# A four-layer graph network: layer 2's accumulators and row products change PSUM tiles, and four edge checks change layers

## The chip, the cores and the metric

The kernel runs on one core of one Trainium2 chip. The metric is the device time of one execution in microseconds; the time before is the median of three runs. A profiled execution gives the trace from which single waits are read.

The engines are called by these names: TensorE (PE in the profile; PEld is its weight load), VectorE (DVE), ScalarE (ACT), GpSimd (POOL) and SyncE (SP), whose queue issues the loads.

## The reference

Node features `x` (4096 x 64) pass through four layers over one adjacency matrix `adj` (4096 x 4096, zeros and ones). Each layer's result is added to its input and normalised by row.

```python
# layer 0: mean over neighbours and self, a linear map of [x, mean], relu, row norm
# layers 1 and 3: hyperbolic attention; for every pair (i, j) a weight
#   sigmoid(left[i] + right[j]) * adj[i, j] times a function of the pair's distance
# layer 2:
support = input @ weight
mask = (adj != 0).astype(support.dtype)
rank = jnp.cumsum(mask, axis=1)
deg = rank[:, -1:]
k = jnp.minimum(deg, float(MAX_NEIGH))
pos = rank - (deg - k)
w = mask * jnp.where(pos > 0, DECAY ** (k - pos), 0.0)
out = w @ support + bias
# after each layer
x = _layernorm(x + layer(x, adj, ...), axis=-1)
```

In layer 2 an edge is thus weighted by two to the minus the number of edges that stand behind it in its row.

## The kernel before

The host hands `adj` over in a blocked order. The 4096 target rows are four groups of 1024 (`GROUPS`, taken in the order 3, 2, 1, 0); the 4096 sources are 32 blocks of 128 (`BLOCKS`, taken from 31 down to 0). `load(s, g)` (L702) brings the edges of group s with two blocks, g from 15 down to 0: one megabyte, 128 partitions by 2 by 1024 fp32, into one of six `edges` buffers. Every layer reads all 64 loads, so the matrix is read four times. The matmuls read the upper bf16 half of each fp32 edge.

**Checks.** The fast path is only valid if every entry is 0 or 1 in the form that it relies on. Each of the 64 loads is therefore checked once, by one VectorE operation over the whole buffer (`check`, L844, 128 x 2048 fp32), which holds the buffer until it is done. `checked_later(s, g)` says in which layer: where it is false, in layer 0 (output `junk`), where it is true, in layer 2 (output in a `t` buffer). Half of the loads of each group go to either layer. Groups 3 and 2 check the loads g = 0, 1, 2, 3, 5, 7, 9, 11 in layer 2; groups 1 and 0 the odd g.

**Row work.** When a group's edges have been summed, the group's 1024 rows go through "row work": the layer's end (`end_0`, `move`, `end_2`), the norm (`norm_rows`) and the preparation of the next layer's operands (`prepare`: casts L931 to L933 on ScalarE, transposes L978, copies out of PSUM L982, the attention product L991, its readers L1001 and L1004, and small operations). These are generators in queues; `tick()` advances them between the blocks of the next group's pass. The order on TensorE and ScalarE in layers 0 and 2 is that of the program (`manual_schedule`); the order on VectorE, GpSimd and SyncE is the planner's.

**PSUM.** [...] After layer 0 the pools are: `aux` (one bank), `z` (three buffers of two banks) and `acc` (one buffer, one bank). Row work takes its PSUM space with `take()`: by turns from `aux` and, where `spare` offers one, from a second place.

**Layer 2.** It has three passes: a wide one over groups 3 and 2 together (`wide_pass`) and two narrow ones over group 1 and group 0 (`narrow_pass`). For each block, `count` (L1641) adds to a running count in a z tile with two matmuls per 512 columns, `weights_of` (L1648) turns the count into weights with ScalarE's exponential, and `add_up` (L1653, wide) or `add` (L1607, narrow) multiplies the weights with the block's supports and accumulates. In a narrow pass each half of 512 rows has its own z tile and its own accumulator, so that one half's exponential runs beside the other half's matmuls. At the end of a pass ScalarE copies the two accumulators to SBUF (L1684), and `end_2` carries them on: transposed or stacked into PSUM (L1134, L1550), read by L1556 and L1560.

Layer 2 takes one of the three z tiles for its whole length:

```python
weighed = [None]
third_z = z_tile()

def of_third(dtype, shape):
    t = third_z[:, W:]
```

The first half of `third_z` is the second accumulator, `accs = [ps.tile([P, W], F32, name="acc"), third_z[:, :W]]`; the second half is row work's second place (`spare.append(of_third)`). The profile names this tile `z`, as it does the other z tiles.

Layer 3 (`attention`, `attend`) follows at once: its loop is L1098, L1101, L1104 on TensorE, the sigmoid L1113 and the square L1116 on ScalarE, L1119 and L1121 on VectorE and the sum L1076 into `acc`.

Of the kernel before, what the change touches and what calls it, by code (L numbers as in the profile page):

```python
# [10 lines left out]
F32 = mybir.dt.float32  # L11
# [8 lines left out]
P = 128  # L20
# [3 lines left out]
W = 512  # L24
# [36 lines left out]
def gnn_stack_kernel(  # L61
# [509 lines left out]
    def stream(fits):  # L571

        with ExitStack() as st:

            def pool(name, bufs=1, **kw):
                return st.enter_context(tc.tile_pool(name=name, bufs=bufs, **kw))
# [7 lines left out]
            GROUPS = tuple(reversed(range(NW)))  # L584
# [31 lines left out]
            def tick(n):  # L616
                for _ in range(n):
                    place[1] += 1
                    mark(False)
                    for queue in queues:  # L620
                        while queue and queue[0][1] <= place[1]:
                            wait = next(queue[0][0], None)
                            if wait is None:
                                queue.pop(0)
                                continue
                            queue[0][1] = place[1] + wait
                            if wait:
                                break
                    mark(True)
# [13 lines left out]
            def need(tag):  # L643
                while tag not in done:
                    assert any(queues), tag
                    tick(1)
# [58 lines left out]

            def checked_later(s, g):

                return g in (0, 1, 2, 3, 5, 7, 9, 11) if s in GROUPS[:2] else g % 2 == 1

            def grp(name, bufs=None):  # L710
                kw = {"bufs": bufs} if bufs else {}
# [2 lines left out]
            def nums(name, n=WB):  # L714
                return row.tile([P, n], F32, name=name)
# [638 lines left out]
            with ExitStack() as lp:  # L1354
                own = lp.enter_context(tc.tile_pool(name="m0_own", bufs=1))
                sb = lp.enter_context(tc.tile_pool(name="m0_sb", bufs=2))
                ps = lp.enter_context(tc.tile_pool(name="m0_ps", bufs=6, space=PSUM))
# [91 lines left out]
                with tc.manual_schedule(engines=FIXED):  # L1449
                    for s in GROUPS:  # L1450
# [3 lines left out]
                        for g in reversed(range(NB // 2)):  # L1454
# [3 lines left out]
                            if not checked_later(s, g):  # L1458
                                check(s, g, a, own.tile([P, 2, WW], BF16, name="junk"))
# [44 lines left out]
            ps = pool("p_ps", 1, space=PSUM)  # L1504

            def z_tile():
                return ps.tile([P, WW], F32, name="z", bufs=3)
# [63 lines left out]
            def wide_pass(two):  # L1571

                zs = [z_tile() for _ in two]

                accs = [ps.tile([P, W], F32, name="acc"), third_z[:, :W]]
                behind, lag = [None, None], []
                for g in reversed(range(NB // 2)):
                    edges = [load_2(s, g) for s in two]
                    need((2, 2 * g // WB))
                    for k in (1, 0):  # L1580
                        j = 2 * g + k
                        w = sb.tile([P, 2, WW], F32, name="sq").bitcast(BF16)[:, :, :WW]
                        for i, edge in enumerate(edges):
                            here = edge[:, k * WW : (k + 1) * WW]
                            count(zs[i], behind[i], here, j, WW)
                            behind[i] = here
                            weights_of(zs[i], WW, w[:, i])
                            if i == 1:
                                for of, acc in enumerate(accs if lag else ()):
                                    add_up(acc, *lag[of])  # L1590
                                lag = [(j, w[:, n, :W], w[:, n, W:]) for n in range(2)]
                            if two[0] != GROUPS[0] or j < BLOCKS[4]:
                                tick(1)
                for of, acc in enumerate(accs):
                    add_up(acc, *lag[of])
                return [[acc] for acc in accs]

            def narrow_pass(s):

                zs = [z_tile() for _ in range(2)]  # L1600
                accs = [ps.tile([P, W], F32, name="acc"), third_z[:, :W]]
                behind, lag = [None, None], [None, None]

                def add(h):
                    if lag[h] is not None:
                        j, w = lag[h]
                        nc.tensor.matmul(  # L1607
                            accs[h], halves[:, j, :], w,
                            start=j == BLOCKS[0], stop=j == BLOCKS[-1],
                        )  # L1610

                for g in reversed(range(NB // 2)):
                    edge = load_2(s, g)
                    for k in (1, 0):
                        j = 2 * g + k
                        w = sb.tile([P, 2, WW], F32, name="sq").bitcast(BF16)[:, 0, :WW]
                        for h in range(2):
                            here = edge[:, k * WW + h * W : k * WW + (h + 1) * W]
                            count(zs[h], behind[h], here, j, W)
                            behind[h] = here  # L1620
                            add(h)
                            part = w[:, h * W : (h + 1) * W]
                            weights_of(zs[h], W, part)
                            lag[h] = (j, part)
                        tick(1)
                for h in range(2):
                    add(h)
                return [accs]

            def load_2(s, g):  # L1630
                a, edge = load(s, g)
                if checked_later(s, g):
                    junk = sb.tile([P, 2, WW], F32, name="t", bufs=3).bitcast(BF16)
                    check(s, g, a, junk[:, 0, :].rearrange("p (b i) -> p b i", b=2))
                return edge

            def count(z, behind, here, j, n):
                for lhs, rhs in ((pass_by, behind), (enter, here)):
                    for h in range(0, n, W):
                        if rhs is not None:  # L1640
                            nc.tensor.matmul(  # L1641
                                z[:, h : h + W], lhs, rhs[:, h : h + W],
                                start=j == BLOCKS[0], stop=True, skip_group_check=True,
                            )

            def weights_of(z, n, w):

                weighed[0] = nc.scalar.activation(w, z[:, :n], AF.Exp, bias=-(OFF_EDGE + CUT) * LN2, scale=-LN2)  # L1648

            def add_up(acc, j, *ws):  # L1650
                for part in range(2):
                    for h, w in enumerate(ws):
                        nc.tensor.matmul(  # L1653
                            acc[h * D : (h + 1) * D, :],
                            halves[:, j, part * D : (part + 1) * D], w,
                            start=j == BLOCKS[0] and part == 0,
                            stop=j == BLOCKS[-1] and part == 1,
                        )

            weighed = [None]  # L1660
            third_z = z_tile()

            def of_third(dtype, shape):
                t = third_z[:, W:]
                if dtype == F16:
                    return t.bitcast(F16)
                n = int(np.prod(shape[1:]))
                if len(shape) == 2:
                    return t[:, :n]
                names = "abc"[: len(shape) - 1]  # L1670
                return t[:, :n].rearrange(
                    "p (%s) -> p %s" % (" ".join(names), " ".join(names)),
                    **dict(zip(names, shape[1:])),
                )

            with tc.manual_schedule(engines=FIXED):
                spare.append(of_third)

                for some in (GROUPS[:2], GROUPS[2:3], GROUPS[3:]):
                    accs = wide_pass(some) if len(some) == 2 else narrow_pass(some[0])  # L1680
                    for s, of in zip(some, accs):
                        sums = [row.tile([P, W], F32, name="sums", bufs=2) for _ in of]
                        for to, acc in zip(sums, of):
                            nc.scalar.copy(to, acc)  # L1684
                        later(end_2(s, sums))
                spare_ends()
# [16 lines left out]
            t, g = nums("m1", 1), nums("g1", 1)  # L1703
# [21 lines left out]

    fits = const.tile([P, 1], F32, name="fits")
    stream(fits)

    n_fit = const.tile([1, 1], I32, name="n_fit")
    with tc.tile_pool(name="fit_ps", bufs=1, space=PSUM) as ps:  # L1730
        t = ps.tile([1, P], F32, name="fit_t")
# [52 lines left out]
```

## Time and profile before

| what | value |
|---|---|
| median of three runs | 1076.47 us (1074.18 to 1076.71) |
| the profiled execution | 1073.46 us, span 1071.7 us |
| mean granted TensorE clock | 0.975 |
| busy: PE, DVE, ACT, POOL | 985.7, 919.6, 754.4, 272.3 us |
| layer 0, about | 0 to 184 us |
| layer 1, about | 184 to 513 us |
| layer 2, about | 513 to 720 us (narrow passes from 610 and from 666) |
| layer 3 and the end, about | 720 to 1072 us |
| a check (L844), layer 0 and layer 2 | 2.28 us each, 32 in either layer |

The span runs from the first to the last instruction of the profiled execution; the execution's own time is 1.8 us longer. Single durations and waits come from that one execution; the time to beat is the median. In lists of waits a line says which engine and line waited, for which engine and line, for how long in total, how often and how long at most. In timelines a line is start, duration, engine, line, operation, output and inputs, and in brackets the idle time before it with what ended it. TensorE's durations overlap, since matmuls are pipelined: the spacing of their starts is what counts.

### The profile page before, as it was taken

The numbers are of one execution on the slowest core, as the hardware profiler recorded it, in microseconds if no ns is written. First come the engines' busy times: TensorE is split into PE (matmuls) and PEld (weight loads), VectorE is DVE, ScalarE is ACT, GpSimd is POOL, SyncE is SP. The second block draws the span as 40 slices with busy tenths as digits, with TensorE's granted clock in tenths as the row PEclk, the third lists the DMA queues.
The fourth block names the chain that finished last, engine by engine and source line by source line (L and its number), as shares of the span: only waits on it lengthen the run. The fifth ranks groups of instructions, "written<-read, shape, count | busy, mean of one in ns | idle before, by whom it ended". The sixth has DMA issues, their size and how long they took to land.

```text
span 1071.7 us, 13656 instructions
## 1 busy us (share of the span) xinstructions
PE 985.7 (92%) x4845; PEld 401.4 (37%) x4845; DVE 919.6 (86%) x1501; ACT 754.4 (70%) x877; POOL 272.3 (25%) x649
## 2 busy tenths in 40 slices
PE   4997998789999999999999989998899999999980
PEld 2454554333333333333333334443333333333320
DVE  7676888999999999999485698829999999999976
ACT  0013122879988889888677778898898888898850
POOL 0011211010044515425500021101102444444162
PEclk9999999989999999999999999999999999999985
DMA  9999999645666656657699979896465666666300
GB/s 340 387 424 356 381 416 377 256 167 197 235 205 227 229 202 210 227 192 240 226 358 324 385 282 342 292 327 223 148 237 194 245 221 209 239 230 229 135 1 24
DMA packets 38580, 271.62 MB, mean 253 GB/s; under 512 B 4710, under 2 KB 4710, under 8 KB 5734
## 3 DMA queue, kind: packets, MB, share of 16 engines
q1 hardware_dynamic: 37728, 270.03, 69.2%
q8 instruction: 40, 0.66, 0.2%
q10 hardware_dynamic: 774, 0.63, 0.2%
q14 instruction: 38, 0.31, 0.1%
HBM read 269.58 MB, written 1.05 MB: 253 GB/s over the span
## 4 chain that ended last, share of the span: by engine, by line
PE 61%; DVE 25%; ACT 6%; DMA 3%; POOL 2%; issue 2%; ACTq 0%; SPq 0%; POOLq 0%; DVEq 0%
PE acc L1076 17%; PE z L1641 9%; PE z L1098 8%; PE z L1104 7%; PE z L1101 7%; DVE t L1119 6%; DVE t L1121 6%; PE acc L1465 4%; DVE junk L844 3%; DMA edges<-in_adj_dram 2%; ACT sq L1648 2%; PE acc L1653 2%; ACT sq L1116 1%; PE z L1653 1%; ACT sig L1113 1%
## 5 line engine op out<-in xcount | busy, mean ns | idle before, releaser
L1119 DVE SCALAR_TENSOR_TENSOR t<-z,sig 128x1024 f32<-128x1024 f32 x256 | 309.8, 1219 | 12.8 <-ACT sq L1116 10.9
L1121 DVE SCALAR_TENSOR_TENSOR t<-sq,t 128x2048 f32<-128x2048 f32 x128 | 295.2, 2307 | 0.2
L1116 ACT ACTIVATE sq<-z 128x1024 f32<-128x1024 f32 x256 | 254.2, 1021 | 56.6 <-PE z L1104 21.6
L1113 ACT ACTIVATE sig<-left_b,right 128x1024 f32<-128x1024 f32 x256 | 286.9, 1149 | 5.3 <-DVE t L1119 4.5
L1076 PE MATMUL acc<-t,xe 128*64 128x512 f32 x1024 | 260.0, 614 | 10.6 <-DVE t L1121 9.7
L1098 PE MATMUL z<-edges,two_i 128*128 128x512 bf16 x512 | 200.9, 392 | 5.5 <-DVE t L1119 5.4
L1104 PE MATMUL z<-dst,src 74*128 74x512 f16 x512 | 194.7, 380 | 0.0
L1101 PE MATMUL z<-lo_hi,hi_lo 128*128 128x512 f16 x512 | 193.8, 378 | 0.0
L1648 ACT ACTIVATE sq<-z 128x512 bf16<-128x512 f32 (+1 forms) x192 | 137.8, 741 | 45.3 <-PE z L1641 44.7
L1076 PEld LDWEIGHTS acc<-t,xe 128*64 128x64 f32 x1024 | 64.3, 137 | 140.5 <-issue 106.0
L1465 PE MATMUL acc<-edges,first 128*128 128x512 bf16 x256 | 80.8, 397 | 17.4 <-DMA edges<-in_adj_dram 17.2
L1098 PEld LDWEIGHTS <-two_i 128*128 128x128 bf16 x512 | 50.3, 98 | 120.5 <-issue 74.5
L1641 PE MATMUL z<-edges,pass_by 128*128 128x512 bf16 x248 | 87.2, 391 | 4.9 <-ACT sq L1648 4.6
L844 DVE SCALAR_TENSOR_TENSOR t<-edges 128x2048 bf16<-128x2048 f32 x32 | 73.0, 2287 | 21.4 <-DMA edges<-in_adj_dram 21.0
L1641 PE MATMUL z<-edges,enter 128*128 128x512 bf16 x256 | 88.8, 389 | 0.0
L844 DVE SCALAR_TENSOR_TENSOR junk<-edges 128x2048 bf16<-128x2048 f32 x32 | 73.1, 2284 | 9.0 <-DMA edges<-in_adj_dram 8.8
L1465 PE MATMUL acc<-edges,third 128*65 128x512 bf16 x256 | 80.4, 396 | 0.0
L1104 PEld LDWEIGHTS <-src 74*128 74x128 f16 x512 | 49.2, 96 | 72.1 <-issue 9.2
L1101 PEld LDWEIGHTS <-hi_lo 128*128 128x128 f16 x512 | 50.2, 98 | 60.6 <-issue 14.6
L901 POOL TENSOR_TENSOR sq<-z 128x512 f32<-128x512 f32 x8 | 16.2, 2024 | 168.4 <-DVE z L900 147.3
L1184 POOL TENSOR_TENSOR w_att<-x,u 128x512 f32<-128x512 f32 x6 | 12.7, 2122 | 139.7 <-ACT u L1179 139.7
L1465 PEld LDWEIGHTS <-first 128*128 128x128 bf16 x256 | 24.3, 98 | 45.1 <-issue 16.2
(402 smaller groups left out, 987.3 us busy)
## 6 DMA issues: line engine op xcount, KB each, us to landing
edges<-in_adj_dram SPq DMA_DIRECT2D x256, 1024.0 KB, 4.9
x<-in_x_dram SPq DMA_DIRECT2D x4, 256.0 KB
out_dram<-x ACTq DMA_DIRECT2D x2, 256.0 KB
out_dram<-x SPq DMA_DIRECT2D x2, 256.0 KB
w_sb<-in_L_gnn_W_dram ACTq DMA_DIRECT2D x1, 32.0 KB, 4.7
w_twice<-in_L_gnn_weight_dram ACTq DMA_DIRECT2D x2, 16.0 KB, 8.7
given<-in_L_gnn_b_dram ACTq DMA_DIRECT2D x1, 0.2 KB
given<-in_L_gnn_bias_dram ACTq DMA_DIRECT2D x1, 0.2 KB
```

What stands on the lines that cost most here:

```text
L844: V.scalar_tensor_tensor(junk, a, 0.0, a, ALU.not_equal, ALU.not_equal, accum_out=odd[:, n : n + 1])
L1076: it = nc.tensor.matmul(acc[h * D : (h + 1) * D, :], xe[:, j, :], t[:, k, h * W : (h + 1) * W], start=j == BLOCKS[0], stop=j == BLOCKS[-1],)
L1098: nc.tensor.matmul(half, two_i, edge[:, at : at + W], start=True, stop=False)
L1101: nc.tensor.matmul(half, hi_lo[:, of], lo_hi[:, to], start=False, stop=False)
L1104: last = nc.tensor.matmul(half, src[:, of], dst[:, to], start=False, stop=True)
L1113: nc.scalar.activation(sig, left_b, AF.Sigmoid, bias=right[:, j : j + 1])
L1116: nc.scalar.activation(sq[:, k], zp, AF.Square, bias=ROOT + OFF, scale=-1.0 / UNIT)
L1119: V.scalar_tensor_tensor(t[:, k], zp, 0.0, sig, ALU.max, ALU.mult)
L1121: V.scalar_tensor_tensor(t, sq, HIGH**2, t, ALU.add, ALU.mult)
L1465: nc.tensor.matmul(accs[h][:m], lhs[:, j, :], edge[:, at : at + W], start=j == BLOCKS[0], stop=j == BLOCKS[-1],)
L1641: nc.tensor.matmul(z[:, h : h + W], lhs, rhs[:, h : h + W], start=j == BLOCKS[0], stop=True, skip_group_check=True,)
L1648: weighed[0] = nc.scalar.activation(w, z[:, :n], AF.Exp, bias=-(OFF_EDGE + CUT) * LN2, scale=-LN2)
```

## The change

Three things are edited. `checked_later` returns for groups 1 and 0 what it returned for groups 3 and 2. Both accumulators of a pass are the two halves of `third_z`. Row work's second place is a tile of its own, `row_bank`, allocated once for layer 2 in the `acc` buffer, and `of_third` hands out views of it.

```diff
             def checked_later(s, g):
 
-                return g in (0, 1, 2, 3, 5, 7, 9, 11) if s in GROUPS[:2] else g % 2 == 1
+                return g in (0, 1, 2, 3, 5, 7, 9, 11)
...
                 zs = [z_tile() for _ in two]
 
-                accs = [ps.tile([P, W], F32, name="acc"), third_z[:, :W]]
+                accs = [third_z[:, :W], third_z[:, W:]]
                 behind, lag = [None, None], []
...
                 zs = [z_tile() for _ in range(2)]
-                accs = [ps.tile([P, W], F32, name="acc"), third_z[:, :W]]
+                accs = [third_z[:, :W], third_z[:, W:]]
                 behind, lag = [None, None], [None, None]
...
             weighed = [None]
             third_z = z_tile()
+            row_bank = ps.tile([P, W], F32, name="acc")
 
             def of_third(dtype, shape):
-                t = third_z[:, W:]
+                t = row_bank
                 if dtype == F16:
                     return t.bitcast(F16)
```

For groups 1 and 0 this means: of layer 2's checks, those of loads 15 and 13 move to layer 0, and of layer 0's, those of loads 2 and 0 move to layer 2. The number of checks in either layer stays 32.

## The prediction

> **What bounds the kernel now.** I read the page for the order of the stages, then the table of stretches for each stage, then the list of waits between 510 and 725 us, and then the timelines of TensorE, VectorE and ScalarE around the waits that looked wrong. Layer 0 ends near 184 us, layer 1 near 513, layer 2 near 720. The change touches layers 0 and 2. The stretches first (length, busy time of PE, PEld, DVE, ACT, POOL, then TensorE clock, DMA share, GB/s): three passes of layer 0, then layer 2's wide pass and its two narrow passes.
>
> ```profile
> 54.00:97.00 43.00, 39.00 (x227) 21.81 (x226) 34.88 (x92) 7.90 (x14) 8.72 (x9) 1.00 0.95 382
> 97.00:141.00 44.00, 39.79 (x241) 22.82 (x241) 35.63 (x104) 11.18 (x19) 6.65 (x9) 1.00 0.96 392
> 141.00:184.00 43.00, 40.77 (x256) 23.89 (x254) 35.87 (x109) 10.24 (x19) 6.80 (x9) 1.00 0.97 395
> 510.00:610.30 100.30, 98.55 (x582) 37.33 (x580) 61.80 (x126) 69.66 (x77) 16.70 (x53) 1.00 0.86 319
> 610.30:666.00 55.70, 49.62 (x251) 22.76 (x248) 49.38 (x177) 43.66 (x75) 10.12 (x16) 0.97 0.87 318
> 666.00:720.30 54.30, 50.60 (x290) 24.57 (x289) 30.41 (x100) 48.11 (x83) 4.75 (x8) 1.00 0.88 313
> ```
>
> Layer 0 is bound by its loads. The wide pass is TensorE back to back. The narrow passes are TensorE's too, but with holes: six matmuls per block at 0.2255 us from start to start are 1.353 us, 43.3 us for 32 blocks, against 54 to 56 us taken; row products and short waits on ScalarE fill most of the rest. The first narrow pass alone has a mean clock under 1.00. The waits of layer 2 (who waited, for whom; total, times, longest) and the place of the largest on TensorE and VectorE:
>
> ```profile
> PE z L1607 <- DVE z L1560: 3.4, 1, 3.4
> PE z L1607 <- ACT lo_hi L982: 0.5, 2, 0.2
> PE z L1607 <- ACT dst L982: 0.4, 2, 0.2
> DVE lr L1001 <- ACT sums L1684: 18.0, 1, 18.0
> ```
>
> ```profile
> 623.01 0.39 PE L1641 MATMUL z<-edges,enter 128*128 128x512 bf16 x1
> 626.85 0.59 PE L1607 MATMUL z<-sq,halves 128*128 128x512 bf16 x1 [3.44 <-DVE z L1560]
> 627.23 0.63 PE L1641 MATMUL z<-edges,pass_by 128*128 128x512 bf16 x1
> ```
>
> ```profile
> 625.96 0.42 DVE L1556 SCALAR_TENSOR_TENSOR z<-z,given_b 128x256 f32<-128x256 f32 x1
> 626.38 0.42 DVE L1560 SCALAR_TENSOR_TENSOR z<-z,given_b 128x256 f32<-128x256 f32 x1
> ```
>
> L1607 adds block sums into the first half of `third_z`; L1560 reads a row product out of the second half. They share no number, yet the add waits for the read. The same holds six more times: L1607 waits for L982's copy exactly where that copy reads a z tile, never where it reads `aux`. In the other direction L1001, reading L991's row product in the second half, starts only after the sums' copy of the first half. So waits follow the whole tile.
>
> **What the Trainium skill says.** "PSUM — Partial Sum Buffer", section "PSUM bank collisions raise a hardware error", wants engines kept apart by bank and quadrant; the two halves are 512 fp32 columns each, a bank each, so these waits are wider than the chip asks. "TensorE: Matmul & The Clock Gate", "What's actually happening", has TensorE at half rate after an idle window of about 3.4 us: the trace agrees, the matmuls after the 3.44 us hole start 0.43 us apart instead of 0.2255. "PSUM", "Engine vs sequencer instructions", calls ScalarE's queue a strict FIFO: here three casts at 633.11 keep the next block's exponential waiting and TensorE idles 1.16 us.
>
> **The change, part by part.** It adds and removes no instruction; it moves two PSUM buffers and four checks.
>
> *Tiles.* Both accumulators now lie in `third_z`, row products in the `acc` bank.
> (1) The hole at 623 goes: 3.44 us, and the slow stretch after it: 626.85 to 630.16 for eight matmuls is 3.31 us, at 0.2255 it is 1.80, so 1.5 us more. TensorE sets the pass here; all 4.9 counts. What is late next: ScalarE's casts (L931 to L933), in a fixed order. With the hole gone they come due at 633.11 less 4.9 to 5.1, about 628.1. They need y, which VectorE finished at 631.47. One check ahead of it (615.16, 2.29 us) moves away, so y is there at about 629.3. ScalarE, and the exponentials queued behind the casts, with TensorE waiting for those, lose about 1.0 us; bounds 0.3 (y took 1.54 us beside a GpSimd product, 0.69 elsewhere) and 3.5 (VectorE's order unchanged).
> (2) The six waits of 0.22 us, 1.35 in all: without them TensorE runs a little ahead into the exponential that stands behind the same copy. I take half, 0.7; bounds 0 and 1.35.
> (3) At the end, lr (723.21) and seven small operations stand ahead of layer 3's first L1119 (724.14), though its sigmoid was ready at about 722.6. The row product was made by about 719. Free of the sums' copy, this 0.9 us falls into VectorE's idle time before 722.6, and VectorE is full from 738 to 760, so 0.9 counts; bounds 0 (ScalarE still sets the second L1119) and 1.4.
> (4) The price: a copy of one accumulator now waits for the last add of the other too. At 610.17 the first copy started some 0.3 us before the other's adds ended; the narrow pass's exponentials follow in ScalarE's order: minus 0.3; at the other two pass ends the copies are late anyway. Bounds 0 and 1.
> The first row product in `acc` comes at about 532, the copy that frees it ends at 518.4, and layer 3's first add into `acc` (730.16) is after the last read: nothing at either end.
>
> *Checks.* Passes 1 and 0 move their checks of loads 15 and 13 from layer 2 to layer 0 and those of loads 2 and 0 the other way, 2.28 us each on both sides. In layer 2 the later ones fall beside work: at 650 to 666 VectorE already checked the next pass's loads 15 and 13 (661.5, 663.7), which now go, and after 704.58 it idled 18 us. They hold no buffer that TensorE is not still reading (SyncE's waits there: 188 us for TensorE, 1.2 for checks). In layer 0 they do hold buffers:
>
> ```profile
> SPq L702 <- DVE junk L844: 60.2, 16, 6.7
> SPq L702 <- PE acc L1465: 10.1, 11, 1.9
> ```
>
> That is SyncE's queue from 97 to 184 us: every later load stands behind a load whose buffer waits for a check. How much of it starves the DMA? The shares above leave 5%, 4% and 3% of 43 or 44 us: 2.2, 1.8 and 1.3 us. Pass 2 already has the new pattern and loses 0.4 to 0.9 us more than the others. So I charge 0.4 + 0.9 = 1.3 us for passes 1 and 0. Against it, the last check of layer 0 (182.14 to 184.36) no longer stands before L1428 (184.57), for which TensorE waited 0.93 us at 185.14: plus 0.9. Net minus 0.4. Bounds: minus 9.1 (four checks of 2.28 us, each delaying a load in full) and plus 1.2 (nothing but the end).
>
> **Sum**: 4.9 - 1.0 + 0.7 + 0.9 - 0.3 - 0.4 = 4.8 us. The profiled execution took 1073.46 us (span 1071.7, 1.8 around it), so 1068.7 on its scale; the median of the runs is 1076.47, 3.0 above that execution, so **1071.7 us**. A measurement of this kernel tells 0.3%, 3.2 us, from no change.
>
> **Rivals.**
> *The wait moves to the casts.* VectorE's work before y is not shortened, for instance because other ready work takes the freed place; y stays at 631.47 and ScalarE waits 3.5 us in place of 1.0. For it: VectorE is busy nearly without a break from 624 to 666. Against: one check less stands ahead. Gain 4.8 - 2.5 = 2.3, 1074.2 us: within 0.3%.
> *Layer 0 starves (slower).* In passes 1 and 0 the checks of loads 15 and 13 come ahead of the previous pass's row work, whose chain runs serially through GpSimd; the checks behind it free their buffers later, and the loads of a load-bound stage come late. Full price 9.1 us: 1071.7 - 0.4 + 9.1 = 1080.4 us. It decides from a loss of about 5.2 us in layer 0 on, and exceeds 0.3% from 8.4. For it: the 60.2 us above. Against it: pass 2, and VectorE's holes of 6.0 us at 94.7 and 3.6 at 141, where a check of load 15 fits.
> *More is gained.* The casts wait 0, layer 0 gets the plus 1.2, lr its 1.4, the short waits their 1.35: 4.8 + 1.0 + 1.6 + 0.5 + 0.65 = 8.6, 1067.9 us.
> *The change does nothing*, if waits did go by bank: the seven waits speak against it; I give it no chance of its own.
>
> **How the numbers follow.** Forecast 0.53, more gained 0.12, casts 0.20, layer 0 0.15. The forecast's own range is 1069.5 to 1074.5; its upper edge, 0.04, belongs to no change. Faster 0.61, same 0.24, slower 0.15. The range goes from 1067.0, below the larger gain, to 1079.0, past the casts and a partly starved layer 0; it leaves out about 0.15.
>
> **What would show it.** Right: no wait of L1607 for L1560 or L982; the first narrow pass near 51 us at clock 1.00; a new ScalarE wait of about 1 us at L931 for y; lr before layer 3's first L1119; DMA share of 0.95 in the passes at 97 and 141 us and no check within 4 us of layer 0's end. Wrong: layer 0 over 3 us longer, the hole at another instruction of the narrow pass, or L1607 still waiting for row work.

## The result, and the profile after

The changed kernel takes 1071.84 us in the median (22 runs, 1067.79 to 1079.21), the kernel before, run beside it, 1076.59 (22 runs). The ratio is 0.996, with a 95% interval of 0.9945 to 0.9974: faster by 0.4%, 2.8 to 5.9 us. A second comparison of the same two kernels gave 0.9967 (0.995 to 0.9983). The profiled execution has a span of 1067.3 us against 1071.7, and both kernels' executions are 1.8 us longer than their spans.

The table of stretches of the changed kernel, in the columns used before. The three passes of layer 0 are cut where they were; the wide pass and the two narrow ones are cut where they now begin and end.

```profile
54.00:97.00 43.00, 38.66 (x223) 21.80 (x225) 35.17 (x93) 7.84 (x14) 8.72 (x9) 1.00 0.96 388
97.00:141.00 44.00, 39.68 (x239) 22.92 (x242) 36.06 (x105) 10.95 (x19) 8.74 (x9) 1.00 0.94 381
141.00:184.00 43.00, 40.38 (x250) 23.67 (x252) 36.53 (x109) 10.50 (x19) 8.59 (x9) 1.00 0.97 395
509.60:610.20 100.60, 98.11 (x572) 37.37 (x582) 59.50 (x124) 69.37 (x77) 16.71 (x53) 1.00 0.85 320
610.20:661.20 51.00, 47.41 (x243) 22.32 (x247) 43.59 (x158) 43.85 (x76) 6.07 (x16) 1.00 0.95 336
661.20:714.90 53.70, 50.05 (x284) 24.63 (x288) 39.33 (x130) 48.01 (x81) 3.46 (x8) 1.00 0.91 324
```

The first narrow pass is where the time came from: 51.0 us at a clock of 1.00, where it took 55.8 at 0.97. The wide pass and layer 0 are nearly what they were; only the pass of layer 0 from 97 us has a lower DMA share, 0.94 against 0.96. All of TensorE's waits between 500 and 720 us, weight loads apart:

```profile
PE z L1641 <- ACT sq L1648: 6.0, 7, 1.4
PE acc L1076 <- DVE t L1121: 1.1, 1, 1.1
PE z L1607 <- ACT sq L1648: 0.5, 2, 0.3
PE acc L1319 <- ACT x_t L1312: 0.2, 1, 0.2
PE aux L1550 <- ACT sums L1685: 0.2, 1, 0.2
```

L1607 waits neither for L1560 nor for L982 any more. What it waits for is its own input, the exponential. VectorE at the place of the old hole:

```profile
621.92 2.29 DVE L844 SCALAR_TENSOR_TENSOR t<-edges 128x2048 bf16<-128x2048 f32 x1
624.26 0.42 DVE L1556 SCALAR_TENSOR_TENSOR z<-acc,given_b 128x256 f32<-128x256 f32 x1
624.67 0.42 DVE L1560 SCALAR_TENSOR_TENSOR z<-acc,given_b 128x256 f32<-128x256 f32 x1
...
626.75 0.69 DVE L928 TENSOR_TENSOR y<-x,ym 128x512 f32<-128x512 f32 x1
627.35 0.69 DVE L900 TENSOR_TENSOR z<-z,n_m 128x512 f32<-128x512 f32 x1
```

The row product now comes from `acc`, and TensorE doesn't wait for the read. In this pass one check stands ahead of `y` where there were two (615.16 and 622.15 in the kernel before), and `y` is done at 627.44, while ScalarE reaches its casts (L931) at 628.31: they don't wait.

The profiled execution's 4.4 us, stage by stage (start of the stage to start of the next, taken from the same instructions in both traces):

| stage | before | after | difference |
|---|---|---|---|
| up to layer 1's first L1119 | 194.02 | 193.66 | -0.36 |
| layer 1, to layer 2's first count | 315.99 | 315.95 | -0.04 |
| wide pass, to the first copy of its sums | 100.16 | 100.59 | +0.43 |
| first narrow pass, to its first copy | 55.84 | 50.95 | -4.89 |
| second narrow pass, to its last add | 53.89 | 53.37 | -0.52 |
| to layer 3's first L1119 | 4.24 | 4.15 | -0.09 |
| layer 3, to its last L1121 | 312.38 | 313.65 | +1.27 |
| rest | 35.18 | 34.98 | -0.20 |

Layer 2 gives 5.0 us. One thing was not foreseen: layer 3 takes 1.27 back, though the change touches nothing there.

### The profile page after: what moved, and what is told of

Read it like the earlier page. It is cut to its first block, busy times and chain, and to the rows that moved or that the text cites. A ratio compares the mean times of both kernels' runs of the same rounds, so it can differ in the third digit from the quotient of the medians.

```text
span 1067.3 us, 13569 instructions
## 1 busy us (share of the span) xinstructions
PE 982.1 (92%) x4760; PEld 403.2 (38%) x4845; DVE 920.2 (86%) x1501; ACT 754.3 (71%) x877; POOL 270.8 (25%) x649
## 4 chain that ended last, share of the span: by engine, by line
PE 66%; DVE 22%; ACT 5%; DMA 2%; POOL 2%; issue 2%; ACTq 0%; SPq 0%; POOLq 0%
PE acc L1076 17%; PE z L1641 11%; PE z L1101 8%; PE z L1098 7%; PE z L1104 7%; DVE t L1119 7%; DVE t L1121 6%; PE acc L1465 6%; PE z L1653 3%; DVE junk L844 2%; PE z L1607 2%; DMA edges<-in_adj_dram 2%; ACT sq L1648 1%; ACT sq L1116 1%; POOL sq L1435 1%
## 5 line engine op out<-in xcount | busy, mean ns | idle before, releaser
L1119 DVE SCALAR_TENSOR_TENSOR t<-z,sig 128x1024 f32<-128x1024 f32 x256 | 309.7, 1218 | 16.9 <-ACT sq L1116 14.9
L1121 DVE SCALAR_TENSOR_TENSOR t<-sq,t 128x2048 f32<-128x2048 f32 x128 | 295.2, 2306 | 0.2
L1098 PE MATMUL z<-edges,two_i 128*128 128x512 bf16 x463 | 181.7, 392 | 5.4 <-DVE t L1119 5.4
L1465 PE MATMUL acc<-edges,first 128*128 128x512 bf16 x241 | 77.9, 400 | 16.5 <-DMA edges<-in_adj_dram 15.9
L1641 PE MATMUL z<-edges,pass_by 128*128 128x512 bf16 x240 | 84.7, 388 | 7.3 <-ACT sq L1648 6.0
L901 POOL TENSOR_TENSOR sq<-z 128x512 f32<-128x512 f32 x8 | 10.2, 1278 | 156.1 <-DVE z L900 144.8
L1607 PE MATMUL z<-sq,halves 128*128 128x512 bf16 x120 | 45.1, 377 | 0.7 <-ACT sq L1648 0.5
```

Of the source, the lines that this page charges most:

```text
L1098: nc.tensor.matmul(half, two_i, edge[:, at : at + W], start=True, stop=False)
L1119: V.scalar_tensor_tensor(t[:, k], zp, 0.0, sig, ALU.max, ALU.mult)
L1121: V.scalar_tensor_tensor(t, sq, HIGH**2, t, ALU.add, ALU.mult)
L1465: nc.tensor.matmul(accs[h][:m], lhs[:, j, :], edge[:, at : at + W], start=j == BLOCKS[0], stop=j == BLOCKS[-1],)
L1641: nc.tensor.matmul(z[:, h : h + W], lhs, rhs[:, h : h + W], start=j == BLOCKS[0], stop=True, skip_group_check=True,)
```

## The experiments

Times are medians; each ratio is to the kernel before run on the same chip, with its 95% interval. "First narrow pass" is from first copy to first copy, as in the table.

**The tiles alone.** The changed kernel with the old `checked_later`.

```diff
-                return g in (0, 1, 2, 3, 5, 7, 9, 11)
+                return g in (0, 1, 2, 3, 5, 7, 9, 11) if s in GROUPS[:2] else g % 2 == 1
```

> Only the tiles change; the checks stay as they were. Theory: the false wait of L1607 goes (3.4 us, and the half-clock stretch behind it, 1.5 us), but VectorE still has the check of 2.28 us ahead of y in the first narrow pass, so ScalarE's casts (L931) wait about 3 us for y where they waited 0 with the whole change. Total gain over the kernel before about 2 us, and the rest of the change's gain needs the checks. Rival: the tiles alone carry it; casts wait under 0.5 us, first narrow pass near 51 us at clock 1.00, gain 4 to 5 us.

Measured: 1078.05 us, ratio 1.0023 (1.0006 to 1.004), a little slower than before. The false waits are gone, but the first narrow pass takes 57.29 us at a clock of 0.94. ScalarE, VectorE and TensorE in this kernel:

```profile
635.21 0.62 ACT L931 CAST ys<-y 128x512 f16<-128x512 f32 x1 [4.74 <-DVE y L928]
```

```profile
616.52 2.28 DVE L844 SCALAR_TENSOR_TENSOR t<-edges 128x2048 bf16<-128x2048 f32 x1
...
623.64 2.29 DVE L844 SCALAR_TENSOR_TENSOR t<-edges 128x2048 bf16<-128x2048 f32 x1
...
630.48 2.29 DVE L844 SCALAR_TENSOR_TENSOR t<-edges 128x2048 bf16<-128x2048 f32 x1
633.64 1.54 DVE L928 TENSOR_TENSOR y<-x,ym 128x512 f32<-128x512 f32 x1
```

```profile
637.41 0.59 PE L1641 MATMUL z<-edges,pass_by 128*128 128x512 bf16 x1 [6.00 <-ACT sq L1648]
```

Three checks stand ahead of `y` where there were two in the kernel before: the planner, which fixes VectorE's order when the program is built, also put the next one there. The casts wait 4.74 us for it, the exponentials behind them in ScalarE's queue wait along, and TensorE idles 6.0 us where it had idled 3.44, and runs its next stretch at half clock. The wait moved and grew. My expectation had the mechanism, but not its size: it gave 3 us and still a gain.

**The checks alone.** The kernel before with the new `checked_later`.

> Only the checks change; accumulators and row products stay in the shared tile. Theory: L1607 still waits for L1560's read, but that read comes one check (2.28 us) earlier, so the hole is about 1.2 us instead of 3.4 and the clock need not fall: gain 2 to 3.5 us, and the six waits of 0.2 us for L982 remain. Layer 0 ends within 0.3 us of where it did. Rival: the hole stays near 3.4 us because VectorE does other ready work first, gain under 0.5 us. Second rival: layer 0 ends over 1 us later.

Measured: 1076.37 us, ratio 1.0009 (0.9985 to 1.0033), no difference that can be told, where 2 to 3.5 us had been expected. First narrow pass 54.85 us, 1.0 less than before:

```profile
PE z L1607 <- DVE z L1560: 2.4, 1, 2.4
```

One of the two checks ahead of the row product went, but VectorE could not close up by all of its 2.28 us, so the hole is 2.37 us and not the expected 1.2, and the clock still halved (627.71 to 631.12). So the parts do not add: -1.0 us for one, +1.5 for the other in the pass, -4.9 together. Each takes away one of two waits that stand one behind the other.

**Which check.** Two versions of the changed kernel move only one of group 1's two checks, load 15's or load 13's:

```diff
-                return g in (0, 1, 2, 3, 5, 7, 9, 11)
+                return g in ((0, 1, 3, 5, 7, 9, 11, 13) if s == GROUPS[2] else (0, 1, 2, 3, 5, 7, 9, 11))
```

> The changed kernel, except that in group 1 only load 15's check goes to layer 0, and load 13's stays in layer 2 (load 2's stays in layer 0). Theory: each check that is put ahead of y in the first narrow pass makes y one check (2.28 us) later; y was 0.9 us early for ScalarE's casts with both moved, so with one moved the casts wait 1.4 us and the first narrow pass takes 52.3 to 53 instead of 50.9; with none moved they waited 4.7. Rival: the effect is all or nothing (VectorE's order flips as a whole): the casts wait 0, or over 4 us.

Measured with only load 15's moved: 1078.36 us, ratio 1.003 (1.0013 to 1.0047); first narrow pass 57.95 us, casts waiting 4.74 us, three checks ahead of `y`, as with the tiles alone. The rival was right: not one check's length per check.

> The changed kernel, except that in group 1 only load 13's check goes to layer 0, and load 15's stays in layer 2 (load 2's stays in layer 0). Theory: load 13's check is the one that stood between the row products and y in the first narrow pass, while load 15's ran in VectorE's free time before them; with 13 moved, VectorE's order there is the changed kernel's (one check ahead of y), the casts wait 0, the first narrow pass takes 50.9 us and the total is within 1 us of the changed kernel. Rival: both moves are needed, the casts wait again: narrow pass over 52 us, total 2 us or more above the changed kernel.

Measured with only load 13's moved (`15` in place of `13` in the line above): 1071.89 us, ratio 0.9968 (0.9955 to 0.9982), first narrow pass 50.96 us, no wait at L931. Load 15's check runs before the row products, while VectorE is waiting anyway. Load 13's stood between them and `y`; with it there and the tiles changed, the planner's order also puts a later check (630.48 with the tiles alone) ahead of `y` instead of behind. Removing this one check takes two out of the way. Why the planner orders them so is not shown.

**Group 1 alone.** Group 0's checks stay as they were.

```diff
-                return g in (0, 1, 2, 3, 5, 7, 9, 11)
+                return g in (0, 1, 2, 3, 5, 7, 9, 11) if s in GROUPS[:3] else g % 2 == 1
```

> The changed kernel, except that group 0's checks stay as they were; only group 1's two checks move. Theory: the gain needs group 1's checks alone, since in the second narrow pass VectorE has 18 us to spare before layer 3: layer 2 within 0.3 us of the changed kernel, total within 1 us of it. Rival: the checks of group 0's loads 15 and 13 fall at the end of the first narrow pass and make ScalarE's casts of the second one late: layer 2 over 1 us longer.

Measured: 1072.4 us, ratio 0.9963 (0.9946 to 0.998); layer 2's passes 100.59, 50.96 and 53.37 us, the changed kernel's to 0.01. Group 0's moved checks do nothing that can be seen.

**No shared tile, but no second place either.** Accumulators in two tiles as before, new checks, row products in `aux` alone:

```diff
-                spare.append(of_third)
```

> Checks as in the changed kernel, accumulators in two tiles as before, and row products in aux alone (the second half of the third z tile is left empty), so no tile is shared. Theory: what counts is that no tile holds both an accumulator and a row product; no wait of L1607 for L1560 or L982, first narrow pass near 51 us, total within 1 us of the changed kernel, that is 4 to 5 us under the kernel before, even if single row products wait longer for aux. Rival: row work needs the second place; with one place its steps come later, ScalarE's copies in their fixed order hold up the exponentials, and the total is 2 us or more above the changed kernel.

Measured: 1072.16 us, ratio 0.996 (0.994 to 0.998). First narrow pass 50.85 us, no wait of L1607 for row work: it is the sharing of the tile that cost, not which buffer holds what. The wide pass takes 2.2 us longer, because one row product waits for `aux`:

```profile
540.40 0.71 PE L1168 MATMUL aux<-centre,sums 128*128 128x130 f32 x4 [2.32 <-DVE sum L1175]
```

**The second place in the wide pass only.** As the last, but `of_third` stays until the first narrow pass:

```diff
+                    if len(some) == 1:
+                        spare.clear()
                     accs = wide_pass(some) if len(some) == 2 else narrow_pass(some[0])
```

> Checks as changed, accumulators in two tiles as before; row products have the second place (half of the third z tile) in the wide pass only, and aux alone in the two narrow passes. Theory: it joins the best of each stage: the wide pass without the 2.3 us wait for aux and with untied copies (100.2 to 100.3 us from first count to first copy, 0.3 to 0.4 under the changed kernel), the first narrow pass at 50.9. Total 0.3 to 0.5 us under the changed kernel, which the timing can't tell from it. Rival: row products begun in the wide pass still sit in the shared tile when the narrow pass starts, and one add waits for them: 1 us or more above the changed kernel.

Measured: 1070.97 us, ratio 0.9955 (0.9938 to 0.9971); first narrow pass 50.62. The wide pass took 100.68, not 100.2 to 100.3: an add waits 0.5 us for `halves` at 568.49, which eats the untied copies' gain. As good as the changed kernel, not measurably better.

**The sums copied later.** The last pass's two copies move into a generator, `copied_late`, which makes them and goes on with `end_2`; it is advanced for the first time behind layer 3's first block.

```diff
                     for s, of in zip(some, accs):
+                        if s == GROUPS[3]:
+                            continue
...
                 spare_ends()
+            later(copied_late(GROUPS[3], accs[0]), wait=1)
```

> The changed kernel, with the last pass's two copies of the sums issued by ScalarE after layer 3's first square instead of ahead of it. Theory: ScalarE's order sets layer 3's first L1119 (it started 0.04 us after that square ended, 4.0 us after lr's work); the square starts about 1.0 us earlier, L1119 too, and layer 3 keeps it: 0.5 to 1.0 us under the changed kernel. Rival: something else comes last there (TensorE's order with the row products), or VectorE gives it back in group 3's pass: no difference, or slower since group 0's row work comes about 2 us later.

Measured: 1071.83 us, ratio 0.9965 (0.995 to 0.9981), the same as the changed kernel. Layer 3's first L1119 does come 0.97 us sooner after the last add:

```profile
718.49 1.23 DVE L1119 SCALAR_TENSOR_TENSOR t<-z,sig 128x1024 f32<-128x1024 f32 x1 [3.04 <-ACT sq L1116]
```

It still waits for the square, which is what sets it. But layer 3 then takes 314.62 us, 0.97 more. The lead is gone with the second L1119, 7.56 us after the last add where it came at 6.10 in the changed kernel: VectorE reads the row product ahead of it, and that product now waits for the later copy. A stretch of TensorE at half clock follows (720.92 to 724.33).

```profile
718.99 2.45 PE L1550 MATMUL aux<-stack,sums 128*128 128x64 f32 x16 [1.10 <-ACT sums L1694]
721.47 0.42 DVE L1556 SCALAR_TENSOR_TENSOR z<-aux,given_b 128x256 f32<-128x256 f32 x1 [1.75 <-PE aux L1550]
```

At the fifth L1119 the two kernels are 0.08 us apart. The rival was right, in its first form: the order with the row products takes the time back.

**The changed kernel again**, with no edit.

> The changed kernel once more, beside the others. Theory: layer 2 takes the same to 0.3 us (205 us from its first count to its last add), and what differs between executions is where TensorE's half-clock stretches fall; the stretch at group 0's row work in layer 3 (1.3 us, absent in the profile of before) comes in most executions. Ratio to the kernel before 0.994 to 0.998. Rival: the stretch in layer 3 was a single accident and layer 3 takes 312.4 us as it did before.

Measured: 1072.26 us, ratio 0.9967 (0.995 to 0.9983). Layer 2's passes are the same to 0.01 us, and layer 3 takes 313.64. Windows of this run around group 0's row work in layer 3:

```profile
758.00:762.00 4.00, 2.13 (x17) 1.37 (x18) 4.00 (x10) 2.67 (x4) 3.39 (x6) 0.83 0.00 0
760.60:764.00 3.40, 3.29 (x17) 1.42 (x14) 3.40 (x10) 2.74 (x3) 0.79 (x1) 0.50 0.00 0
```

A stretch of 3.4 us at clock 0.50 follows two idle times of TensorE. Such a stretch is in twelve of the fourteen profiles of this study (in one of them it is twice as long); the kernel before's is one of the two without it.

**Fewer checks in layer 0.** The changed kernel without layer 0's 16 checks of groups 1 and 0.

```diff
-                            if not checked_later(s, g):
+                            if not checked_later(s, g) and s in GROUPS[:2]:
```

> The changed kernel with layer 0's 16 checks of groups 1 and 0 left out (they are done nowhere; the array of results is zeroed first), so its output's guard covers fewer entries. Theory: layer 0 is bound by its loads and the checks only use VectorE's spare time; without them layer 0 ends within 1 us of where it did, and the total is less than 2 us lower. Rival: loads queue behind buffers that wait for a check, and the 66 us for which SyncE waited for checks between 97 and 184 us cost real time: layer 0's two last passes shorten by 4 us or more.

Measured: 1066.84 us (6 runs), ratio 0.9919 (0.9891 to 0.9947), about 5 us under the changed kernel. Layer 1's first L1119 comes at 190.71 us; it came at 193.66 and 194.58 in the two profiles of the changed kernel. Layer 0's last two passes, first without those checks, then with them (the changed kernel run again):

```profile
97.00:141.00 44.00, 42.62 (x257) 24.51 (x260) 18.83 (x88) 13.29 (x22) 4.29 (x9) 1.00 1.01 424
141.00:178.00 37.00, 35.76 (x220) 20.69 (x223) 19.18 (x92) 6.45 (x13) 5.08 (x9) 1.00 1.01 426
```

```profile
97.00:141.00 44.00, 40.45 (x245) 23.04 (x244) 36.43 (x105) 11.30 (x20) 8.74 (x9) 1.00 0.94 383
141.00:178.00 37.00, 34.63 (x198) 19.07 (x197) 33.30 (x104) 6.04 (x12) 8.59 (x9) 1.00 1.00 415
```

The theory was wrong and the rival right about the cause: checks in layer 0 do hold up loads, 424 GB/s without against 383 with them. The trace shows 3 to 4 us of the gain in layer 0; where the rest lies was not settled. A check costs some 0.3 us on average (5 us over 16), an eighth of its length. How long SyncE waited for checks was no measure of that, since without them it waits as long for TensorE, with the DMA full:

```profile
SPq L702 <- PE acc L1466: 62.9, 32, 5.3
```

With this price, moving the same number in and out should cost nothing, while moving them out for good could gain.

**Moving them out.** The version with the second place in the wide pass only, and more checks in layer 2: three more of group 0's (loads 8, 6, 4), then also loads 6 and 4 of groups 3 and 2.

```diff
-                return g in (0, 1, 2, 3, 5, 7, 9, 11)
+                return g in (0, 1, 2, 3, 5, 7, 9, 11) or (s == GROUPS[3] and g in (4, 6, 8))
```

> The version with the second place in the wide pass only, and three more of group 0's checks (loads 8, 6, 4) moved from layer 0 to layer 2, where VectorE idles 9 us or more at the end of the second narrow pass. Theory: leaving out 16 checks in layer 0 took about 5 us off, some 0.3 us each, so a check in layer 0 does cost time in the load-bound passes; three fewer are worth about 1 us, and layer 2 keeps its length (its last add within 0.3 us). Ratio to the kernel before about 0.994 to 0.995. Rival: layer 2's end gets later than it saves, since checks now stand ahead of lr and layer 3's first L1119: no gain or a loss.

Measured: 1071.37 us (9 runs), ratio 0.9949 (0.9925 to 0.9973). Layer 2 keeps its lengths (100.47, 50.61, 53.44), so nothing is lost at the end; the last pass of layer 0 moves 416 GB/s, where it moved 383 in the version that this one starts from and 395 in the changed kernel. The gain itself is within the spread: the version that it starts from took 1070.97 us.

```diff
-                return g in (0, 1, 2, 3, 5, 7, 9, 11) or (s == GROUPS[3] and g in (4, 6, 8))
+                return g in (0, 1, 2, 3, 5, 7, 9, 11) or (s == GROUPS[3] and g in (4, 6, 8)) or (s in GROUPS[:2] and g in (4, 6))
```

> As the version with three more, and four more checks of groups 3 and 2 (loads 6 and 4 of each) in layer 2's wide pass, where VectorE idles about 11 us before the first narrow pass. Theory: seven checks less in layer 0 at some 0.3 us each, about 2 us; VectorE's order ahead of y in the first narrow pass stays (one check), so that pass takes 50.6 to 51 us. Ratio to the kernel before about 0.993. Rival: groups 3 and 2's checks in layer 0 cost nothing, as their passes have buffers to spare, so no more than with three; or the wide pass gets longer because its loads' buffers now wait for checks.

Measured: 1069.2 us (6 runs), ratio 0.9938 (0.9913 to 0.9962), the lowest of the versions that compute everything, though its interval overlaps the changed kernel's. The wide pass grew to 101.99 us, so the second rival holds in part: 1.3 us of what layer 0 gains goes there. Its profile is also one of the two without the half-clock stretch in layer 3 (312.39 us).

## Why the prediction was right

The total came out as predicted, 1071.84 against 1071.7. The mechanism was right; that the number is so close is in part luck, because misses cancelled: the 1.0 us that the casts were to lose and didn't makes up for the 0.8 us that lr was to give and didn't.

**Bound and mechanism: right.** Waits go by the whole tile. Two ways of ending the sharing (accumulators together, or row work elsewhere) both take L1607's waits for row work away, and with the sharing kept (checks alone) they stay.

**(1) 4.9 less 1.0: the first number right, the second wrong.** Of the pass's 4.89 us the hole and its slow stretch make 4.94 and two short waits 0.45; against that, the casts' own hold-up of TensorE grew from 1.16 to 1.37, and one wait of 0.32 for an exponential is new. The casts were to wait 1.0 us and waited 0. The failed step is "y is there at about 629.3": I took one check away and kept the rest of VectorE's order. VectorE in the kernel before:

```profile
622.15 2.28 DVE L844 SCALAR_TENSOR_TENSOR t<-edges 128x2048 bf16<-128x2048 f32 x1
...
628.38 0.69 DVE L953 TENSOR_TENSOR xw<-x,g 128x512 f32<-128x512 f32 x1
...
629.05 0.69 DVE L900 TENSOR_TENSOR z<-z,n_m 128x512 f32<-128x512 f32 x1
...
629.93 1.54 DVE L928 TENSOR_TENSOR y<-x,ym 128x512 f32<-128x512 f32 x1
```

With the change, L953 and L900 come behind `y`, and `y` takes 0.69 us instead of 1.54, since GpSimd's product of what L900 writes (629.88 to 630.92 here) no longer runs beside it. So `y` was done at 627.44, 1.9 us sooner than I reckoned. The experiments with one check show the two outcomes of the planner's order: casts that wait 4.74 us, or not at all. My bound for an unchanged order, 3.5 us, was too small because the order didn't stay as it was: with the tiles alone a third check came ahead of `y`. The rival in which the wait moves to the casts was more dangerous than I priced it: it made the tiles alone slower than before.

**(2) 0.7 for the six short waits: right.** The second narrow pass lost four of them, 0.89 us, and became 0.52 shorter. The rest went into exponentials that come 0.32 us late, as argued.

**(3) 0.9 for lr: wrong, 0.09.** VectorE in the changed kernel at the start of layer 3:

```profile
713.65 0.21 DVE L1001 TENSOR_REDUCE lr<-acc 128x16 f32<-128x48 f32 x1 [9.10 <-PE acc L991]
...
718.67 1.22 DVE L1119 SCALAR_TENSOR_TENSOR t<-z,sig 128x1024 f32<-128x1024 f32 x1 [4.01 <-ACT sq L1116]
```

lr is out of the way by 5 us, as foreseen. But L1119 waits for ScalarE's square of the same z tile, not for its sigmoid alone; I had read "its sigmoid was ready" as enough. The square ends where it did, since ScalarE takes table load, sigmoid, copies and square in the same order. The Trainium skill offers a reason on a page that I had used for something else: "PSUM — Partial Sum Buffer", section "PSUM bank collisions raise a hardware error", says that the compiler's scheduler orders any two engines on one bank and quadrant, two readers included. The traces agree with such an order and don't show its reason: in the changed kernel and with the later copies, L1119 starts 0.04 and 0.03 us after the first square ends. In the kernel before it is 0.04 us too, but there VectorE's own small operations end at the same time.

**(4) -0.3 for the tied copies: right, -0.43.** The first copy of the wide pass waits 0.76 us for the adds, and 0.33 wherever the accumulators have tiles of their own.

**Checks in layer 0, -0.4: not to be told.** The +0.9 did not come: the offset of -0.36 at the end of layer 0 was already -0.26 at the check at 92 us, ahead of any moved one, and TensorE still waited 0.83 us for L1428 at the end (0.93 before), with no check ahead of it: L1428 was now late for its own input, L1421's product. The -1.3 came from reading pass 2's lower DMA share as the price of the pattern. The pass from 97 us did fall from 392 GB/s to 381; the six profiles with the changed kernel's checks have 381 to 384 there, the two with the old checks 392 and 393, about 1 us of the pass by my estimate. The pass from 141 us shows no such split (383 to 398 against 388 and 395). In the six profiles layer 1's first L1119 comes between 193.66 and 198.35 us, so a price of a microsecond can't be read from one of them. The rival in which layer 0 starves had a true cause, at about an eighth of its full price for an average check.

**Not in the sum: layer 3's 1.27 us.** It is the half-clock stretch above. The kernel before probably has it too in many executions: the tiles alone and the checks alone, its nearest relatives, have it in their profiles (313.27 and 313.30 us), and its own profile happened to miss it. If so, the 4.4 us between the two spans are too low by about that much. How much of it is in the medians is not known.

## What to carry to other kernels

Where two waits stand one behind the other, price the change with the second one's owner's whole queue in view: taking the first away alone can make things worse, since the planner may reorder the engine that feeds the second. Ask of each check, copy or cast not how long it is but whose input it stands in front of; one operation of 2.28 us in the wrong place was worth 7 us of a pass here, another of the same kind nothing. And before a difference of a microsecond between two profiles is put down to the change, compare stage by stage with a third profile of the same kernel: TensorE's half-clock stretches come and go by themselves.

## What the runs showed of the hardware

TensorE's clock changes on a fixed grid. In the changed kernel it falls or rises at 196.18, 199.59, 230.31, 237.14, 759.38 and 762.79 us, which are multiples of 3.413 us apart to 0.01; in the kernel before the same holds for 200.01, 230.73, 626.68 and 630.09. The Trainium skill says so ("TensorE: Matmul & The Clock Gate", "What's actually happening": a free-running window of 3413 ns). What I had not expected, having counted a whole idle window in the prediction, is how little idle time is enough. In the changed kernel TensorE idles 1.48 and 1.10 us with 0.62 us of work between, all but 0.06 us of it inside the window that ends at 759.38, and the next window is at half clock:

```profile
757.39 0.62 PE L978 MATMUL aux<-ident,ys 128*128 128x128 f16 x8 [1.48 <-DVE ys L947]
759.11 0.80 PE L978 MATMUL aux<-ident,ys 128*128 128x128 f16 x8 [1.10 <-ACT hi_lo L982]
```

In the kernel before the same two idle times (761.39 to 762.87 and 763.49 to 764.59) lie on both sides of the grid's 763.21, and the clock stays. With the checks alone, one hole of 2.37 us inside one window was enough too; the single holes of 1.1 to 1.4 us in layer 2 were not. So 2.4 us of idle time in a window of 3.41 did it, and where the window's edge falls counts. The fourteen traces together, from 40 to 1030 us, say more: all 42 windows at full clock with over 1.9 us without a matmul were followed by one at half clock, and of some 3900 with less only 15 were. Eight of these had 1.5 to 1.9 us; the other seven, with 0 to 1.2 us, are filled mainly by L1420, L1421 and L1550, matmuls of 64 or 65 columns, so idle time is not all that counts. (A matmul's end is modelled in the profile, and no run tests what the narrow ones do.)

One core drew 424 to 427 GB/s from memory from 97 to 184 us when no buffer waited for a check, with the DMA engines' share at 1.01.
